# A two-layer graph network: weights split by two engines, and the first four steps in another order

## The chip, the core and the metric

The kernel runs on one core of a Trainium2 chip. The metric is the device time of one launch in microseconds (us), here the median of 3 runs. A core has five engines that run side by side: TensorE (PE, matrix products; its weight loads are listed as PEld), VectorE (DVE), ScalarE (ACT), GpSimd (POOL) and SyncE (SP), which in this kernel only issues DMA transfers. Each engine takes its instructions in the order of the program and waits on semaphores for what other engines produce.

## The reference

For each of N = 128 graphs g with C = 128 nodes and D = 512 features (cut to what matters):

```python
h = relu(layernorm(x))                              # [C, 512]
H = (adj != 0); w = adj[0]                          # incidence, weights of the hyperedges
Dn = 1 / (H @ w); Be = 1 / H.sum(axis=0)            # 0 where the sum is 0
def conv(x, W, b): return Dn * (H @ (Be * (H.T @ (x @ W.T)))) + b
n = layernorm(relu(conv(h, W1, b1))) * gamma + beta # [C, 1024]
x = x + conv(n, W2, b2) + h                         # layer 0
h = relu(layernorm(x))
agg = (adj @ h) / max(adj.sum(-1), 1e-6)
out = x + relu(concat(h, agg) @ W.T)                # layer 1, W is [512, 1024]
```

x is [128, 128, 512], adj [128, 128, 128], all float32. The products with W1, W2 and W must be nearly exact in float32.

## The kernel before

All weights stay in SBUF. [...]each operand of the three large products is split: h is the operand scaled down a little, l what is left (times 4096 in a weight), and d the difference of the two (l - h in a weight). A product is then h.h + l.l in one PSUM bank (`pm`) and d.d in another (`pd`), 8 or 16 matmuls and 4 or 8 more, combined on the way out. The weights, twelve chunks of 128x1024 (some halved), are split once, in the first steps; the raw weights lie in buffers that the loop will use later (`t1`, `h1`, `A` and so on). `DOWN` is 1 - 2^-13, `ONE_UP` 1 + 2^-12. Blank lines are left out here.

```python
class Chunks:
    def __init__(self, w, k, n, tag):
        self.raw = (pool if tag in "rA" else left).tile([P, n, 512], FP, tag=tag, name="raw")
        self.h, self.l, self.d = (w[m][:, k : k + n].bitcast(FR) for m in "hld")
    def high(self):
        copy(self.h, self.raw, AF.Copy, scale=DOWN)
    def low(self, eng):
        eng.tensor_tensor(self.l, self.raw, self.h, SUB)
    def scale(self, eng=nc.scalar):
        if eng is nc.scalar:
            copy(self.l, self.l, AF.Copy, scale=4096.0)
        else:
            eng.tensor_scalar(self.l, self.l, 4096.0, None, MUL)
    def rest(self, eng):
        eng.tensor_tensor(self.d, self.l, self.h, SUB)

W2_TILES = {6: (1, "h1"), 7: (1, "h2"), 0: (1, "h3"), 1: (1, "A"), 2: (2, "t1"), 4: (2, "t2")}
def load_w2(k):
    n, tag = W2_TILES[k]
    c = RAW[2, k] = Chunks(w2, k, n, tag)
    for j in range(Q):
        nc.sync.dma_start(
            out=c.raw[B * j : B * (j + 1)],
            in_=w2t.rearrange("(j k a) o -> j a k o", j=Q, a=B)[j, :, k : k + n])
def scale_w2(k):
    for i in range(W2_TILES[k][0]):
        t = RAW[2, k].raw[:, i, :]
        nc.vector.tensor_scalar(t, t, vector_of(1, k + i), None, MUL)

def beta_row(k):
    if not BETA:
        BETA[0] = small_bank("pc")
    n = W2_TILES[k][0]
    for i in range(n):
        nc.tensor.matmul(BETA[0], vector_of(0, k + i).to_broadcast([P, P]), RAW[2, k].raw[:, i, :],
                         start=(k + i == 6), stop=(k + i == 5))
```

Per graph: `incidence` and `node_matrix` make the graph operators, `mean_operator` that of layer 1.

```python
def mean_operator(g):
    a = ADJ.pop(g)
    deg = pool.tile([P, 1], FP, tag="deg", name="deg", bufs=2)
    nc.vector.tensor_reduce(deg, a, AX.X, ADD)
    nc.vector.tensor_scalar(deg, deg, EPS_DEG, None, MAX)
    nc.vector.reciprocal(deg, deg)
    nc.vector.tensor_scalar(a, a, deg, None, MUL)
    ADJ[g] = a

def incidence(g):
    HT[g] = at = pool.tile([P, P], FP, tag="ht", name="adjt")
    nc.vector.transpose(at, ADJB.pop(g))
    SB[g] = sb = pool.tile([P, P + 1], FP, tag="sb", name="sb")
    nc.vector.tensor_copy(sb[:, P : P + 1], at[:, 0:1])
    nc.vector.tensor_scalar(at, at, 0.0, None, ALU.not_equal)
    cnt = pool.tile([P, 1], FP, tag="cnt", name="cnt", bufs=2)
    nc.vector.tensor_reduce(cnt, at, AX.X, ADD)
    nc.vector.tensor_scalar(cnt, cnt, 1.0, None, MAX)
    nc.vector.reciprocal(cnt, cnt)
    nc.vector.tensor_scalar(sb[:, :P], at, cnt, None, MUL)
def node_matrix(g):
    ps = small_bank("ps_s")
    nc.tensor.matmul(ps[:, : P + 1], HT.pop(g), SB.pop(g), start=True, stop=True)
    S[g] = pool.tile([P, P], FP, tag="s", name="s", bufs=4)
    copy(S[g], ps[:, :P], AF.Copy)
    inv = pool.tile([P, 1], FP, tag="inv", name="inv", bufs=2)
    w = ps[:, P : P + 1]
    nc.vector.tensor_scalar(inv, w, TINY, None, MAX)
    nc.vector.reciprocal(inv, inv)
    DN[g] = dn = pool.tile([P, 2], FP, tag="dinv", name="dinv", bufs=6)
    nc.vector.scalar_tensor_tensor(dn[:, 0:1], w, 0.0, inv, ALU.is_gt, MUL)
    nc.vector.tensor_scalar(dn[:, 1:2], dn[:, 0:1], ONE_UP, None, MUL)
...
def product(left, w, k0, kk, main, name, between=None):
    wr = [w[m].bitcast(FR) for m in "hld"]
    pm, pd = bank(name + "m"), bank(name + "d")
    for i in range(2):
        for k in range(kk):
            nc.tensor.matmul(pm, left[i](k), wr[i][:, k0 + k, :], start=(i == 0 and k == 0),
                             stop=(i == 1 and k == kk - 1))
    main(pm)
    if between:
        between()
    for k in range(kk):
        nc.tensor.matmul(pd, left[2](k), wr[2][:, k0 + k, :], start=(k == 0),
                         stop=(k == kk - 1), skip_group_check=True)
    return pd
...
def conv1_weights(g, half):
    if half == 0:
        R[g] = pool.tile([P, DH], FP, tag="r", name="r")
    cols = HALVES[half]
    r, dn = R[g][:, cols], DN[g]
    PR[g, half] = product(Z[g], w1, KD * half, KD,
                          lambda pm: copy(r, pm, AF.Copy, scale=dn[:, 1:2]), "r")
def conv1_out(g, half):
    cols = HALVES[half]
    r, dn = R[g][:, cols], DN[g]
    nc.vector.scalar_tensor_tensor(r, PR.pop((g, half)), dn[:, 0:1], r, MUL, ADD)
    nc.gpsimd.tensor_tensor(r, r, b1_bc[:, cols], ADD)
```

The left operands of conv2 and layer 1 are turned by a round trip through DRAM (`n_scratch` to `nb`, `h_scratch` to `hb`: one store, four loads) and a transpose on VectorE; then ScalarE makes h, GpSimd l, VectorE d (`split_high`). The order is written by hand. One step of the loop works on several graphs at once; `do(f, g)` runs f for graph g if there is such a graph:

```python
def step(s, extra={}, done=()):
    def do(f, g, *a):
        do(aggregate, s - 3)
    do(layer1_low, s - 3)
    do(conv2_bias, s - 2)
    do(conv1_weights, s, 0)
    do(conv1_out, s, 0)
    do(layer1_rest, s - 3)
    do(residual, s + 1)
    do(mean_operator, s)
    do(mean_out, s)
    do(conv1_weights, s, 1)
    do(conv1_out, s, 1)
    do(conv2_nodes, s - 2)
    do(conv2_out, s - 2)
    do(inner_turn, s - 1)
    do(conv1_nodes, s + 1)
    do(layer1_sums, s - 2)
    do(inner_high, s - 1)
    do(inner_low, s - 1)
    do(scales, s - 2, 3)
    do(mean_in, s)
    do(conv1_high, s + 1)
    do(layer1_mean, s - 3)
    do(layer1_norm, s - 2)
    do(layer1_trip_out, s - 2)
    do(conv1_low, s + 1)
    do(conv1_rest, s + 1)
    do(layer1_mean_out, s - 3)
    do(layer1_self, s - 3)
    do(inner_sums, s)
    do(inner_rest, s - 1)
    do(layer1_trip_in, s - 2)
    do(layer1_self_main, s - 3)
    do(scales, s, 2)
    do(incidence, s + 2)
    do(inner_norm, s)
    do(inner_out, s)
    do(finish, s - 3)
    do(load_adjb, s + 4)
    do(load_adj, s + 1)
    do(inner_in, s)
    do(load_x, s + 3)
    do(x_sums, s + 2)
    do(layer1_turn, s - 2)
    do(scales, s + 2, 1)
    do(conv2_main, s - 1)
    do(x_norm, s + 2)
    do(conv2_weights_out, s - 1)
    do(layer1_high, s - 2)
    do(mean_transpose, s)
    do(node_matrix, s + 2)
```

(Inside conv2_weights, between its two banks, stands `aggregate` of s - 3; it is called through `between`, and without conv2_weights by itself.) The first steps are written out instead:

```python
def split_w3(*cs):
    for c in cs:
        RAW[3, c].high()
        RAW[3, c].low(nc.vector)
    for c in cs:
        RAW[3, c].scale()
        RAW[3, c].rest(nc.gpsimd)

def head():
    copy(eps_root, eps, AF.Sqrt)
    load_x(0)
    load_adjb(0, nc.scalar)
    for half in range(2):
        for i in range(2):
            load_w1(half, i, nc.sync)
    load_affine()
    load_bias(b1_bc, b1)
    load_adjb(1)
    load_x(1)
    load_bias(b2_bc, b2)
    for k in (6, 7, 0, 1):
        load_w2(k)
    load_adj(0)
    x_sums(0)
    incidence(0)
    scales(0, 1)
    RAW[1, 0, 0].high()
    x_norm(0)
    node_matrix(0)
    RAW[1, 0, 1].high()
    RAW[1, 0, 0].low(nc.vector)
    RAW[1, 0, 1].low(nc.gpsimd)
    conv1_nodes(0)
    RAW[1, 0, 0].scale()
    conv1_high(0)
    RAW[1, 0, 1].scale()
    conv1_low(0)
    conv1_rest(0)
    RAW[1, 0, 0].rest(nc.vector)
    RAW[1, 0, 1].rest(nc.gpsimd)
    RAW[1, 1, 0].high()
    RAW[1, 1, 1].high()
    RAW[1, 1, 0].low(nc.vector)
    RAW[1, 1, 1].low(nc.gpsimd)
    RAW[1, 1, 0].scale()
    conv1_weights(0, 0)
    RAW[1, 1, 1].scale()
    RAW[1, 1, 0].rest(nc.vector)
    RAW[1, 1, 1].rest(nc.gpsimd)
    residual(0, nc.vector)
    conv1_out(0, 0)
    load_x(2)
    load_w2(2)
    load_w2(4)
    incidence(1)
    x_sums(1)
    conv1_weights(0, 1)
    node_matrix(1)
    scales(1, 1)
    x_norm(1)
    conv1_out(0, 1)
    load_adjb(2)
    load_adjb(3)
    incidence(2)
    for k in (6, 7, 0, 1):
        beta_row(k)
    conv1_nodes(1)
    conv1_high(1)
    for k in (2, 4):
        beta_row(k)
    for k in (6, 7, 0, 1):
        scale_w2(k)
    inner_sums(0)
    conv1_low(1)
    conv1_rest(1)
    residual(1, nc.vector)
    scales(0, 2)
    inner_norm(0)
    inner_out(0)
    for k in (2, 4):
        scale_w2(k)
    beta_out()
    node_matrix(2)
    for k in W2_TILES:
        RAW[2, k].high()
        RAW[2, k].low(nc.vector)
        RAW[2, k].scale(nc.vector)
        if k != 4:
            RAW[2, k].rest(nc.gpsimd)
    mean_operator(0)
    inner_in(0)
    mean_out(0)
    load_adj(1)
    mean_in(0)
    load_w3(0, "h1")
    load_w3(1, "h2")
    load_w3(2, "h3")
    load_x(3)
    load_adjb(4)
    conv1_weights(1, 0)
    conv1_out(1, 0)
    x_sums(2)
    conv1_weights(1, 1)
    scales(2, 1)
    x_norm(2)
    conv1_out(1, 1)
    inner_turn(0)
    inner_high(0)
    inner_low(0)
    conv1_nodes(2)
    conv1_high(2)
    RAW[2, 4].rest(nc.vector)
    inner_rest(0)
    conv2_weights(0, lambda: None)
    inner_sums(1)
    conv1_low(2)
    conv1_rest(2)
    scales(1, 2)
    inner_norm(1)
    inner_out(1)
    mean_operator(1)
    residual(2)
    incidence(3)
    node_matrix(3)
    conv2_main(0)
    conv2_weights_out(0)
    conv2_bias(0)
    mean_out(1)
    load_adj(2)
    x_sums(3)
    scales(3, 1)
    x_norm(3)
    inner_in(1)
    mean_transpose(0)
    mean_in(1)
    split_w3(0, 1, 2)
    load_w3(3, "h1")
    load_w3(4, "h2")
    load_w3(5, "h3")
    load_x(4)
    load_adjb(5)
    # then step(2) with the rest of W3, and step(3), step(4), ... up to step(N + 2)
```

Of the kernel before, what the change touches and what calls it, by code (L numbers as in the profile page):

```python
# [23 lines left out]
def gnn_kernel(  # L24
# [33 lines left out]
    P = 128  # L58
# [35 lines left out]
    def parts(tag):  # L94
        return {m: const.tile([P, KH, 512], FP, name=tag + m) for m in "hld"}

    w1, w2, w3 = parts("w1"), parts("w2"), parts("w3")
    RAW = {}

    class Chunks:  # L100


        def __init__(self, w, k, n, tag):
            self.raw = (pool if tag in "rA" else left).tile([P, n, 512], FP, tag=tag, name="raw")
            self.h, self.l, self.d = (w[m][:, k : k + n].bitcast(FR) for m in "hld")

        def high(self):
            copy(self.h, self.raw, AF.Copy, scale=DOWN)

        def low(self, eng):  # L110
            eng.tensor_tensor(self.l, self.raw, self.h, SUB)

        def scale(self, eng=nc.scalar):
            if eng is nc.scalar:
                copy(self.l, self.l, AF.Copy, scale=4096.0)  # L115
            else:
                eng.tensor_scalar(self.l, self.l, 4096.0, None, MUL)  # L117

        def rest(self, eng):
            eng.tensor_tensor(self.d, self.l, self.h, SUB)  # L120


    def load_w1(half, i, queue):
        src = w1t.rearrange("(k p) h -> p k h", p=P)
        c = RAW[1, half, i] = Chunks(w1, KD * half + 2 * i, 2, ("r", "t1", "t2", "t3")[2 * half + i])
        queue.dma_start(out=c.raw, in_=src[:, 2 * i : 2 * i + 2, HALVES[half]])

    W2_TILES = {6: (1, "h1"), 7: (1, "h2"), 0: (1, "h3"), 1: (1, "A"), 2: (2, "t1"), 4: (2, "t2")}

    def load_w2(k):  # L130
        n, tag = W2_TILES[k]
        c = RAW[2, k] = Chunks(w2, k, n, tag)
        for j in range(Q):
            nc.sync.dma_start(
                out=c.raw[B * j : B * (j + 1)],
                in_=w2t.rearrange("(j k a) o -> j a k o", j=Q, a=B)[j, :, k : k + n])

    def scale_w2(k):
        for i in range(W2_TILES[k][0]):
            t = RAW[2, k].raw[:, i, :]  # L140
            nc.vector.tensor_scalar(t, t, vector_of(1, k + i), None, MUL)

    def load_w3(c, tag):
        src = wt.rearrange("(n j k a) o -> n j a k o", n=2, j=Q, a=B)
        RAW[3, c] = r = Chunks(w3, c, 1, tag)
        for j in range(Q):
            nc.sync.dma_start(out=r.raw[B * j : B * (j + 1), 0], in_=src[1 - c // KD, j, :, c % KD])
# [5 lines left out]
    def load_affine():  # L153
        for j in range(Q):
            for i, v in enumerate((beta, gamma)):
                nc.gpsimd.dma_start(
                    out=gb[B * j : B * (j + 1), i].rearrange("a (l m) -> a l m", m=2),
                    in_=v.rearrange("(l a) (j m) -> j a l m", a=B, j=Q)[j])

# [6 lines left out]
    BETA = {}  # L166

    def beta_row(k):
        if not BETA:
            BETA[0] = small_bank("pc")  # L170
        n = W2_TILES[k][0]
        for i in range(n):
            nc.tensor.matmul(BETA[0], vector_of(0, k + i).to_broadcast([P, P]), RAW[2, k].raw[:, i, :],
                             start=(k + i == 6), stop=(k + i == 5))
# [76 lines left out]
    def mean_transpose(g):  # L251
        anb = ANT[g]
        ANT[g] = pool.tile([P, P], FP, tag="ant", name="ant", bufs=4)
        nc.vector.transpose(ANT[g], anb)
# [29 lines left out]
    def x_sums(g):  # L284
        H0[g] = pool.tile([P, D], FP, tag="B", name="h0")
        sums((1, g), X[g], H0[g], D)
        spread((1, g), X[g], H0[g], D)
# [14 lines left out]
    def conv1_high(g):  # L302
        Z[g] = z = left.tile([P, 3, KD, P], FP, tag="z", name="z")
        h, l, d = (z[:, i].rearrange("p k c -> p (k c)").bitcast(FR) for i in range(3))
        pz = PZ.pop(g)
        copy(h, pz, AF.Copy, scale=DOWN)  # L306

# [11 lines left out]
    def conv1_rest(g):  # L319
        PZ.pop(g)[1]()  # L320
        z = Z[g].bitcast(FR)
        Z[g] = [lambda k, i=i: z[:, i, k, :] for i in range(3)]


    def product(left, w, k0, kk, main, name, between=None):
        wr = [w[m].bitcast(FR) for m in "hld"]
        pm, pd = bank(name + "m"), bank(name + "d")
        for i in range(2):
            for k in range(kk):
                nc.tensor.matmul(pm, left[i](k), wr[i][:, k0 + k, :], start=(i == 0 and k == 0),  # L330
# [4 lines left out]
        for k in range(kk):  # L335
            nc.tensor.matmul(pd, left[2](k), wr[2][:, k0 + k, :], start=(k == 0),  # L336
# [6 lines left out]
    def conv1_weights(g, half):  # L343
        if half == 0:
            R[g] = pool.tile([P, DH], FP, tag="r", name="r")
        cols = HALVES[half]
        r, dn = R[g][:, cols], DN[g]
        PR[g, half] = product(Z[g], w1, KD * half, KD,
                              lambda pm: copy(r, pm, AF.Copy, scale=dn[:, 1:2]), "r")  # L349

    def conv1_out(g, half):
# [3 lines left out]
        nc.gpsimd.tensor_tensor(r, r, b1_bc[:, cols], ADD)  # L355
# [38 lines left out]
    def split_high(key, a, tags):  # L394
# [8 lines left out]
        def low():  # L403
            SPLIT[key] = part(*l)
            nc.gpsimd.tensor_tensor(SPLIT[key], a, h, SUB)  # L405
# [15 lines left out]
    def inner_low(g):  # L421
        NT[g][0]()
# [331 lines left out]
```

## Time and profile before

| | |
|---|---|
| median of 3 runs | 2566.73 us (2566.22 to 2567.98) |
| span of the profiled execution | 2563.8 us |
| PE busy | 2495.7 us (97%), 11024 matmuls |
| DVE busy | 2062.3 us (80%) |
| ACT busy | 1865.6 us (73%) |
| POOL busy | 1367.8 us (53%) |
| mean granted clock of PE | 0.989 |
| DMA | 311.71 MB, mean 122 GB/s |

A line of the profile's groups reads: line of the program, engine, operation, what it writes <- what it reads, shape and type, xcount | busy us in all and mean ns of one | idle time of the engine just before, and what ended it. `L111` is `Chunks.low`, `L120` is `Chunks.rest`, `L330` and `L336` are the two matmuls of `product`. A line of waits reads: engine, its tile and line <- the engine, tile and line that it waited for: us in total, times, longest.

### The profile page before, as it was taken

What the parts mean: (1) busy time and instruction counts of PE and PEld (TensorE: products, weight loads), DVE (VectorE), ACT (ScalarE), POOL (GpSimd) and SP (SyncE); (2) the same over time, 40 slices, a digit from 0 to 9 for tenths busy, and PEclk for the clock granted to TensorE, in tenths of its full rate; (3) what the DMA queues carried; (4) which work ended last, traced back from release to release, by engine and by line L of the source; (5) the groups of instructions that cost most, each with busy time, mean ns of one, the idle gap of its engine ahead of it and who ended that gap; (6) DMA issues with size and microseconds to landing.
All of it is one profiled execution on the core that took longest, in us unless ns stands there. A gap on an engine that the chain in (4) does not pass through costs nothing.

```text
span 2563.8 us, 38459 instructions
## 1 busy us (share of the span) xinstructions
PE 2495.7 (97%) x11024; PEld 1984.0 (77%) x11024; DVE 2062.3 (80%) x4519; ACT 1865.6 (73%) x3872; POOL 1367.8 (53%) x921
## 2 busy tenths in 40 slices
PE   4799999999999999999999999999999999999997
PEld 3578778778778778778778777787787777877875
DVE  7788888888888887888888878888888888888874
ACT  4677777777777777777777777777777777777773
POOL 4555455455455455555555555555555555555552
PEclk8899999999999999999999999999999999999998
DMA  3343443343343343343443343334343344343332
GB/s 117 115 128 117 128 127 116 125 128 115 128 127 117 128 127 117 125 128 118 124 129 117 120 130 122 119 126 126 119 130 122 117 130 125 116 130 125 116 124 67
DMA packets 410292, 311.71 MB, mean 122 GB/s; under 512 B 177376, under 2 KB 341216, under 8 KB 410080
## 3 DMA queue, kind: packets, MB, share of 16 engines
q1 hardware_dynamic: 409248, 309.19, 38.5%
q8 instruction: 87, 1.43, 0.2%
q14 instruction: 125, 1.02, 0.1%
q10 hardware_dynamic: 576, 0.07, 0.0%
q0 software_dynamic: 256, 0.01, 0.0%
HBM read 166.47 MB, written 142.61 MB: 121 GB/s over the span
## 4 chain that ended last, share of the span: by engine, by line
PE 93%; DVE 2%; ACT 2%; DMA 1%; issue 1%; POOL 1%; SPq 0%; ACTq 0%; DVEq 0%; POOLq 0%
PE gm L330 17%; PE rm L330 17%; PE bm L330 9%; PE am L330 9%; PE rd L336 9%; PE gd L336 9%; PE bd L336 4%; PE py L443 4%; PE ad L336 4%; PE pz L299 4%; PE ad L492 4%; PE ps_s L273 1%; DMA hb<-h_scratch 0%; DVE w2l L117 0%; DMA adjb<-in_adj_dram 0%
## 5 line engine op out<-in xcount | busy, mean ns | idle before, releaser
L405 POOL TENSOR_TENSOR hl<-ht,hh 128x512 fp32r<-128x512 f32 x128 | 165.3, 1291 | 1029.4 <-ACT hh L401 595.9
L217 ACT ACTIVATE h<-x_t 128x512 f32<-128x512 f32 x256 | 161.5, 631 | 343.8 <-DVE x_t L446 327.3
L355 POOL TENSOR_TENSOR r<-r,b_bc 128x512 f32<-128x512 f32 x256 | 386.0, 1508 | 9.2 <-DVE r L354 7.0
L405 POOL TENSOR_TENSOR nl<-nt,nh 128x1024 fp32r<-128x1024 f32 x128 | 308.7, 2411 | 100.3 <-ACT nh L401 99.3
L349 ACT ACTIVATE r<-rm,dinv 128x512 f32<-128x512 f32 x256 | 174.6, 683 | 226.1 <-PE rm L330 226.1
L336 PE MATMUL gd<-w2d,nd 128*128 128x512 f32 x1024 | 307.7, 443 | 3.6 <-DVE nd L410 3.6
L330 PE MATMUL rm<-w1h,z 128*128 128x512 f32 x1024 | 289.5, 405 | 1.4 <-ACT z L306 1.4
L336 PE MATMUL rd<-w1d,z 128*128 128x512 f32 x1024 | 276.5, 391 | 2.2 <-POOL w1d L120 2.2
L330 PE MATMUL rm<-w1l,z 128*128 128x512 f32 x1024 | 276.7, 392 | 2.0 <-ACT w1l L115 2.0
L336 PEld LDWEIGHTS gd<-w2d,nd 128*128 128x128 f32 x1024 | 193.2, 189 | 97.8 <-issue 31.0
L330 PE MATMUL gm<-w2h,nh 128*128 128x512 f32 x1024 | 255.7, 392 | 7.4 <-ACT nh L401 7.4
L330 PE MATMUL gm<-w2l,nl 128*128 128x512 f32 x1024 | 254.6, 391 | 0.0
L228 ACT ACTIVATE h<-x_t,rs 128x512 f32<-128x512 f32 x256 | 208.3, 814 | 32.5 <-DVE rs L224 27.8
L330 PEld LDWEIGHTS gm<-w2h,nh 128*128 128x128 f32 x1024 | 193.8, 189 | 48.2 <-ACT nh L401 7.9
L312 DVE SCALAR_TENSOR_TENSOR z<-z 128x512 fp32r<-128x512 f32 x128 | 226.2, 1768 | 4.4
L330 PEld LDWEIGHTS rm<-w1l,z 128*128 128x128 f32 x1024 | 193.1, 189 | 45.4 <-ACT w1l L115 2.9
L336 PEld LDWEIGHTS rd<-w1d,z 128*128 128x128 f32 x1024 | 192.2, 188 | 45.6 <-POOL w1d L120 3.1
L330 PEld LDWEIGHTS gm<-w2l,nl 128*128 128x128 f32 x1024 | 192.7, 188 | 40.5 <-POOL nl L405 0.4
L330 PEld LDWEIGHTS rm<-w1h,z 128*128 128x128 f32 x1024 | 183.8, 190 | 33.3 <-ACT z L306 1.7
L410 DVE SCALAR_TENSOR_TENSOR hd<-hh,hl 128x512 fp32r<-128x512 f32 x128 | 198.0, 1547 | 4.7 <-POOL hl L405 4.7
L309 DVE TENSOR_TENSOR z<-pz,z 128x512 fp32r<-128x512 f32 x128 | 88.6, 692 | 136.5 <-ACT z L306 136.5
L354 DVE SCALAR_TENSOR_TENSOR r<-rd,dinv,r 128x512 f32<-128x512 f32 x256 | 190.8, 745 | 6.4 <-ACT r L349 1.9
(96 smaller groups left out, 5700.8 us busy)
## 6 DMA issues: line engine op xcount, KB each, us to landing
n_scratch<-r SPq DMA_DIRECT2D x128, 512.0 KB, 2.6
nb<-n_scratch SPq DMA_DIRECT2D x512, 128.0 KB, 2.8
x_t<-in_x_dram SPq DMA_DIRECT2D x128, 256.0 KB, 3.2
h_scratch<-h SPq DMA_DIRECT2D x128, 256.0 KB, 2.0
hb<-h_scratch SPq DMA_DIRECT2D x512, 64.0 KB, 2.0
out_dram<-x_t SPq DMA_DIRECT2D x128, 256.0 KB, 2.0
adj_t<-in_adj_dram SPq DMA_DIRECT2D x128, 64.0 KB, 1.9
an_scratch<-adj_t SPq DMA_DIRECT2D x128, 64.0 KB, 1.7
```

The lines of the kernel that those rows point to most:

```text
L217: copy(junk, src, func, accum_out=sm)
L228: copy(dst, src, func, bias=rs[:, 1:2], scale=rs[:, 0:1])
L299: nc.tensor.matmul(z[:, k * P : (k + 1) * P], H0[g][:, k * P : (k + 1) * P], S[g], start=True, stop=True)
L312: nc.vector.scalar_tensor_tensor(d, h, 2.0**-12, l, MUL, SUB)
L330: nc.tensor.matmul(pm, left[i](k), wr[i][:, k0 + k, :], start=(i == 0 and k == 0), stop=(i == 1 and k == kk - 1))
L336: nc.tensor.matmul(pd, left[2](k), wr[2][:, k0 + k, :], start=(k == 0), stop=(k == kk - 1), skip_group_check=True)
L349: lambda pm: copy(r, pm, AF.Copy, scale=dn[:, 1:2]), "r")
L354: nc.vector.scalar_tensor_tensor(r, PR.pop((g, half)), dn[:, 0:1], r, MUL, ADD)
L355: nc.gpsimd.tensor_tensor(r, r, b1_bc[:, cols], ADD)
L405: nc.gpsimd.tensor_tensor(SPLIT[key], a, h, SUB)
L410: nc.vector.scalar_tensor_tensor(t, h, 2.0**-12, low, MUL, SUB)
L443: nc.tensor.matmul(py, S.pop(g), G.pop(g), start=True, stop=True)
```

## The change

It does five things. The weights are split by ScalarE and VectorE alone; before, GpSimd shared that work. ScalarE multiplies W1 and W3 by 4096 before they are split (for W2 the factor is put into gamma), and VectorE takes l from h and raw in one instruction. A raw half weight lies where its third part d will be, so that it takes no buffer of the loop. The order of the first four steps is new: `head` now reaches into what was step 3, and gives to VectorE some biases and lows that GpSimd does in the loop. In the loop the mean operator of layer 1 is made two steps later, and its buffer is 2 deep instead of 4. The aim is to keep TensorE fed in the first steps.

The diff, cut to its core (cuts are marked; in `head` only the lines of after are shown, as the old head stands above):

```diff
-class Chunks: ...
+class Half:
+    def __init__(self, name):
+        self.name = name
+        self.raw = const.tile([P, KD, 512], FP, tag=name + "d", name=name + "r")
+        self.h, self.l = (const.tile([P, KD, 512], FP, tag=name + m, name=name + m).bitcast(FR)
+                          for m in "hl")
+        self.d = None
+    def up(self, i, eng=nc.scalar):
+        t = self.raw[:, 2 * i : 2 * i + 2]
+            copy(t, t, AF.Copy, scale=4096.0)
+            eng.tensor_scalar(t, t, 4096.0, None, MUL)
+    def high(self, i):
+        c = slice(2 * i, 2 * i + 2)
+        copy(self.h[:, c], self.raw[:, c], AF.Copy, scale=DOWN / 4096.0)
+    def low(self, i):
+        c = slice(2 * i, 2 * i + 2)
+        nc.vector.scalar_tensor_tensor(self.l[:, c], self.h[:, c], -4096.0, self.raw[:, c], MUL, ADD)
+    def rest(self, i, eng=nc.vector):
+        if self.d is None:
+            self.d = const.tile([P, KD, 512], FP, tag=self.name + "d", name=self.name + "d").bitcast(FR)
+        c = slice(2 * i, 2 * i + 2)
+        eng.tensor_tensor(self.d[:, c], self.l[:, c], self.h[:, c], SUB)
+w1, w2, w3 = ([Half(f"w{n}{i}") for i in range(2)] for n in (1, 2, 3))
...
-def load_w2(k): (six tiles, 4 transfers each)
+def load_w2(half): (4 transfers for 4 rows of 512)
+def scale_w2(k, eng): (on ScalarE or VectorE, in place)
...
 def load_affine(): ...
+    nc.gpsimd.tensor_scalar(gb[:, 1], gb[:, 1], 4096.0, None, MUL)
...
-    ANT[g] = pool.tile([P, P], FP, tag="ant", name="ant", bufs=4)
+    ANT[g] = pool.tile([P, P], FP, tag="ant", name="ant", bufs=2)
...
-def conv1_high(g): ...
+def conv1_high(g, early=False): (if early, z lies in h1, h2, h3)
...
 def step(s, ...):
     do(conv1_weights, s, 0)
+    do(conv1_main, s, 0)     (the ACT copy of r, before inside conv1_weights)
...
-    do(mean_operator, s); do(mean_out, s)
+    do(mean_operator, s - 2); do(mean_out, s - 2)
...
-    do(mean_in, s)
+    do(mean_in, s - 2)
...
-    do(load_adj, s + 1)
+    do(load_adj, s - 1)
...
-    do(mean_transpose, s)
+    do(mean_transpose, s - 2)
...
 def head():
     copy(eps_root, eps, AF.Sqrt)
     load_adjb(0, nc.scalar)
     for half in range(2):
         for i in range(2):
+            load_w1(half, i)
     load_affine()
+    load_x(1)
+    load_adjb(1)
     load_bias(b1_bc, b1)
+    for half in range(2):
+        load_w2(half)
     load_bias(b2_bc, b2)
+    load_x(2)
+    load_adjb(2)
     load_adj(0)
     x_sums(0)
+    w1[0].up(0)
+    w1[0].high(0)
+    scales(0, 1)
+    x_norm(0)
+    w1[0].up(1)
+    w1[0].high(1)
     incidence(0)
+    w1[0].low(0)
     node_matrix(0)
     conv1_nodes(0)
+    w1[0].low(1)
+    w1[1].up(0)
+    w1[1].high(0)
+    w1[0].rest(0)
     conv1_high(0)
     conv1_low(0)
     conv1_rest(0)
+    w1[0].rest(1)
+    w1[1].up(1)
+    w1[1].high(1)
+    w1[1].low(0)
+    x_sums(1, "A")
+    scales(1, 1)
+    w1[1].low(1)
+    incidence(1)
+    x_norm(1)
     conv1_weights(0, 0)
+    conv1_main(0, 0)
+    for k in range(2):
+        beta_row(k)
+        scale_w2(k, nc.scalar)
+    w1[1].rest(0)
+    w1[1].rest(1)
+    node_matrix(1)
+    conv1_nodes(1)
     conv1_weights(0, 1)
+    conv1_high(1, True)
     conv1_low(1)
     conv1_rest(1)
+    conv1_main(0, 1)
+    for k in range(2, 4):
+        beta_row(k)
+    conv1_weights(1, 0)
+    conv1_out(0, 0, nc.vector)
+    for k in range(2, 4):
+        scale_w2(k, nc.vector)
+    for i in range(2):
+        w2[0].high(i)
+    conv1_out(0, 1, nc.vector)
+    load_adjb(3)
+    load_w3(0)
+    load_w3(1)
+    for k in range(4, 8):
+        beta_row(k)
+    conv1_weights(1, 1)
+    inner_sums(0)
+    w2[0].low(0)
+    w2[0].low(1)
+    residual(0)
+    for k in range(4, 6):
+        scale_w2(k, nc.vector)
     scales(0, 2)
     inner_norm(0)
     inner_out(0)
+    for k in range(6, 8):
+        scale_w2(k, nc.vector)
+    incidence(2)
+    x_sums(2)
+    scales(2, 1)
+    w2[1].high(0)
+    w2[1].low(0)
+    x_norm(2)
+    node_matrix(2)
+    conv1_nodes(2)
+    w2[1].high(1)
+    w2[1].low(1)
+    conv1_high(2)
+    conv1_low(2)
+    conv1_rest(2)
+    conv1_main(1, 0)
+    conv1_main(1, 1)
     beta_out()
     inner_in(0)
     load_x(3)
     load_adjb(4)
+    load_x(4)
+    load_adjb(5)
     inner_turn(0)
     inner_high(0)
+    w3[0].up(0)
+    w3[0].high(0)
+    conv1_out(1, 0, nc.vector)
+    inner_low(0, nc.vector)
+    conv1_out(1, 1, nc.vector)
+    conv1_weights(2, 0)
+    conv1_weights(2, 1)
+    for i in range(2):
+        w2[0].rest(i)
+    residual(1)
     inner_sums(1)
+    w2[1].rest(0)
     scales(1, 2)
     inner_norm(1)
     inner_out(1)
+    w3[0].up(1)
+    w3[0].high(1)
+    w2[1].rest(1)
+    inner_rest(0)
+    conv2_weights(0, lambda: None)
     residual(2)
     incidence(3)
     x_sums(3)
     scales(3, 1)
     x_norm(3)
+    node_matrix(3)
+    conv1_nodes(3)
+    conv2_main(0)
+    conv2_weights_out(0)
+    conv2_bias(0, nc.vector)
+    conv2_nodes(0)
+    conv1_high(3, True)
+    conv1_main(2, 0)
+    conv1_main(2, 1)
+    conv1_low(3)
+    conv1_rest(3)
+    conv1_weights(3, 0)
+    conv1_weights(3, 1)
     inner_in(1)
+    conv2_out(0)
+    conv1_out(2, 0, nc.vector)
+    layer1_sums(0)
+    inner_turn(1)
+    conv1_out(2, 1, nc.vector)
+    inner_high(1)
+    scales(0, 3)
+    inner_low(1, nc.vector)
+    layer1_norm(0)
+    layer1_trip_out(0)
+    w3[0].low(0)
+    w3[1].up(0)
+    w3[1].high(0)
+    inner_rest(1)
+    conv2_weights(1, lambda: None)
+    inner_sums(2)
+    w3[0].low(1)
+    scales(2, 2)
+    conv2_main(1)
+    inner_norm(2)
+    conv2_weights_out(1)
+    conv2_bias(1, nc.vector)
+    conv2_nodes(1)
+    conv2_out(1)
+    inner_out(2)
+    layer1_trip_in(0)
+    mean_operator(0)
+    mean_out(0)
+    load_adj(1)
+    w3[1].low(0)
+    w3[1].up(1)
+    w3[1].high(1)
+    w3[1].low(1)
+    residual(3)
+    incidence(4)
+    x_sums(4)
+    scales(4, 1)
+    layer1_turn(0)
+    layer1_high(0)
+    layer1_low(0, nc.vector)
+    x_norm(4)
+    node_matrix(4)
+    layer1_rest(0)
+    w3[0].rest(0)
+    w3[0].rest(1)
+    inner_in(2)
+    mean_in(0)
+    w3[1].rest(0)
+    w3[1].rest(1)
     mean_transpose(0)
+    load_adjb(6)
+    load_x(5)
 with tc.manual_schedule():
     head()
+    step(3, done=(conv1_weights, conv2_bias, conv2_nodes, conv2_out,
+                  layer1_low, layer1_rest))
+    for s in range(4, N + 3):
         step(s)
```

## The prediction

> **What bounds the kernel now.** The page comes first: the busy line and the 40 slices of 64 us.
>
> ```profile
> PE 2495.7 (97%) x11024; PEld 1984.0 (77%) x11024; DVE 2062.3 (80%) x4519; ACT 1865.6 (73%) x3872; POOL 1367.8 (53%) x921
> ...
> PE   4799999999999999999999999999999999999997
> ...
> PEclk8899999999999999999999999999999999999998
> ```
>
> TensorE is the bound, and only slices 1, 2 and the last show holes. The waits of TensorE from 120 to 2500 us are one line:
>
> ```profile
> PE py L443 <- POOL g L439: 0.4, 1, 0.4
> ```
>
> So a step of the loop lasts as long as its matmuls: the first `rm` starts at 1012.59 and, one step later, at 1031.84, 19.25 us for one g. What the other engines save there is worth nothing. I cut the first 120 us into stages (columns: stage, length, then PE, PEld, DVE, ACT, POOL busy us with counts, clock, DMA share, GB/s):
>
> ```profile
> 10.00:30.00 20.00, 11.26 (x34) 7.49 (x34) 15.72 (x20) 11.72 (x18) 13.42 (x5) 0.96 0.58 163
> 30.00:48.00 18.00, 16.32 (x52) 9.83 (x52) 15.03 (x39) 10.90 (x20) 3.26 (x3) 0.85 0.09 33
> 48.00:64.00 16.00, 2.02 (x8) 1.78 (x8) 15.72 (x18) 3.89 (x9) 10.60 (x6) 0.53 0.18 49
> 64.00:80.00 16.00, 13.45 (x53) 10.25 (x53) 9.97 (x28) 10.11 (x22) 7.06 (x4) 0.94 0.49 143
> 80.00:100.00 20.00, 8.95 (x29) 6.78 (x28) 15.72 (x20) 14.45 (x30) 15.69 (x11) 0.75 0.33 86
> 100.00:120.00 20.00, 16.89 (x65) 12.85 (x65) 12.56 (x31) 11.00 (x24) 11.57 (x9) 0.83 0.37 110
> ```
>
> From 48 to 64 us VectorE is full (15.72 of 16) and TensorE has 2 us of work. The waits of TensorE up to 122 us name the rest:
>
> ```profile
> PE ps_s L273 <- DVE sb L268: 17.0, 4, 9.9
> PE pz L299 <- ACT h L228: 15.2, 1, 15.2
> PE gm L330 <- ACT nh L401: 7.4, 1, 7.4
> PE gd L336 <- DVE nd L410: 3.6, 1, 3.6
> PE rd L336 <- POOL w1d L120: 2.2, 2, 1.6
> ```
>
> The 15.2 us before `pz` is a chain: ScalarE's `h` waited for `rs` on VectorE, and `rs` stood in VectorE's program behind six W2 chunks (44 to 58 us).
>
> How much can be won? At full clock a 128x512 matmul costs 0.2275 us (four in 0.91). Work up to the start of `gm` of g=2 at 120.04: conv1 of g=0 to 3, conv2 of g=0 and 1, layer 1 of g=0 are 24 matmuls each, 7 x 5.46 = 38.2; beta rows 16 records x 0.45 = 7.2; five `pz` at 0.9 = 4.5; two `py` at 0.9 = 1.8; five `ps_s` 1.2. Together 52.9. So 120.0 - 52.9 = **67 us are lost in the head**. The change removes no matmul, so all it can save lies in these 67 us. The first `ps_s` at 9.88 us waits for the first adjacency, which comes no earlier, so over 57 us is out of reach, and 51 us (2%) would need a head with almost no hole.
>
> [...]
>
> ```profile
> 16.40 3.01 POOL L120 TENSOR_TENSOR w1d<-w1l,w1h 128x1024 fp32r<-128x1024 f32 x1 [1.17 <-DMA raw<-in_w2t_dram]
> ```
>
> ```profile
> 17.30 3.19 DVE L111 TENSOR_TENSOR w1l<-raw,w1h 128x1024 fp32r<-128x1024 f32 x1
> ```
>
> GpSimd ends at 19.41, VectorE at 20.49, 1.08 later; alone the same instruction takes 1.22 (at 11.79). [...] Here the first four `rm` at 14.64 us took 2.07, later ones 1.07[...].
>
> **The change part by part.** Durations are the uncontended ones of the head, start to start: VectorE 128x1024 1.2, 128x512 0.68; ScalarE 0.97 and 0.55.
>
> 1. *Splitting.* GpSimd lost 17 instructions to splitting (2 low, 15 rest; 33 us busy: 6.5+5.7+6.9+3.2+10.9). [...] ScalarE multiplies W1 and W3 by 4096 before, not between, the parts: the same 0.97 each, but the old chain low, scale, rest (VectorE to ScalarE and back) becomes high, low, rest. For W2, 4096 rides on gamma: the 4.6+4.3 us of VectorE scaling at a mean of 1.14 and 2.17 fall away.
>
> 2. *VectorE's new head,* up to the mean_transpose that ends it: 12 chunks x (low+rest) = 24 x 1.2 = 28.8; six W2 rows x 0.42 = 2.5; five incidences x 1.7 = 8.5 (8.04 to 9.74); five node matrices x 0.75 = 3.75; nine scales x 0.4 = 3.6; conv1 splits 4 x 1.35 = 5.4; six conv1_out with bias (now VectorE's) x 1.35 = 8.1; turn, low, rest of two inner operands 6 x 1.2 = 7.2; conv2 out and bias 2 x 1.33 = 2.7; conv2_out 2 x 0.7 = 1.4; layer 1 turn, low, rest 2.0; mean operator, transpose, beta_out 1.8. **Sum 75.8 us.** ScalarE, summed likewise, has 59, TensorE 46.6 up to `pz` of g=4. VectorE is thus the bound of the new head: 8 (adjacency lands) + 75.8 = 84 us at the earliest.
>
> 3. *Its idle time.* I walked the new order by hand, each instruction after the later of its engine and its input. VectorE waits for W1's second high, for the beta rows ahead of the W2 scaling (a few us around 28 to 34), for ScalarE's sums ahead of scales, and for the n round trip (store 2.6, four issues 1.7, load 2.8 = 7.1 us, mostly filled). That adds 8: 92.
>
> 4. *Contention left.* GpSimd keeps four residuals of 2 x 1.26 us = 10 us in the head, and starts each as soon as its input is there. If half of it blocks VectorE: 5. **Head end at about 97.** What then stands between it and `gm` of g=2 is two conv1_out, a mean operator, inner_turn (3.5), ScalarE's high (1.0), some 5 us: `gm` of g=2 starts at about **102**, against 120.0. On the way I expect the first `gm` at 50 (64.0), `py` of g=0 at 63 (79.3), `gm` of g=1 at 72 (88.6), `pz` of g=4 at 90 (113.7). TensorE has those 5 us filled with layer 1 of g=0.
>
> 5. *Order within a step, the mean operators.* The load, the operator and the transpose move by two steps but keep their places in a step: the same instructions, the transpose now one step ahead of its `aggregate`, before three. Nothing in the loop; in the last two steps they are extra, about 1 us of VectorE each, where VectorE waits 1 to 4 us at a time: under 1 us.
>
> Sum: 120 - 102 = 18 saved, less 1.3 for the first steps after the head and the tail: 16.7. 2566.7 - 16.7 = **2550 us**.
>
> **Rivals.** *A: VectorE takes over as the bound and eats the gain.* It gets the biases, lows and rests of GpSimd. For: it is busy 86.5 of 120 us already, and 15.72 of 16 in the worst stage. Against: much of that is blocked time (3.19 for 1.22, 1.37 for 0.43). If all 10 us of residuals and 15 us of idling fall on it, `gm` of g=2 starts at 114: 2561. *B: the DMA round trips and the queue set the head.* The load of the sixth blocked adjacency waits for a buffer that incidence(3) frees, and inner_out(1) stands behind it in the same queue; g=1's turn would come late, perhaps 3 to 6 us: 2553 to 2556. *C: the loop suffers.* Each 0.1 us per step is 12.8 us; against it speaks the 0.4 us of waits in 2380 us and VectorE at 82% there. 2565 to 2580, unlikely. *D: it goes as planned,* VectorE never idle, nothing blocked: head 86, `gm` at 91: 2538.
>
> **Range and chances.** D and A bound it: 2539 to 2562. More than 2% faster (below 2515) would need 51 of the 57 us within reach, when VectorE's sum alone forbids more than some 30; over 2% slower needs the loop to break. So 0.01 / 0.98 / 0.01; that it is faster at all I put at 0.9.
>
> **What would show it.** Right: GpSimd busy 15 to 20 us of the first 95 (66 of 120 before), no 3 us VectorE split, VectorE over 80% busy from 10 to 95 us with TensorE waiting mainly for VectorE, `gm` of g=2 near 102, step still 19.25. Wrong: TensorE waiting for `nb` or `hb` landings (B), `gm` of g=2 beyond 112 (A), a new wait in the loop (C).

## The result and the profile after

| | before | after |
|---|---|---|
| median of 6 runs | 2566.94 us | 2545.1 us |
| ratio, 95% interval | 1 | 0.9918, 0.9905 to 0.9931 |
| span of the profiled execution | 2563.8 us | 2541.1 us |
| `gm` of g=0 starts at | 64.03 | 48.87 |
| `py` of g=0 | 79.27 | 63.72 |
| `gm` of g=1 | 88.60 | 71.90 |
| `pz` of g=4 | 113.67 | 88.57 |
| `gm` of g=2 | 120.04 | 99.70 |

The change won 21.8 us, 0.8%; foretold were 16.7, 2550 us with a range of 2539 to 2562. The mark that the prediction aimed at is the start of `gm` of g=2, in before (first line) and in after:

```profile
120.04 1.98 PE L330 MATMUL gm<-w2h,nh 128*128 128x512 f32 x8
```

```profile
99.70 1.20 PE L337 MATMUL gm<-w20h,nh 128*128 128x512 f32 x4 [1.65 <-ACT nh L408]
```

A line of this kind has the start in us, the length in us, and in brackets how long the engine stood idle before it and what ended that. `fp32r` in such lines is the type float32r, `FR` in the code. The page of after, busy time and slices:

```profile
PE 2490.4 (98%) x11024; PEld 1982.9 (78%) x11024; DVE 2057.7 (81%) x4523; ACT 1866.5 (73%) x3864; POOL 1324.0 (52%) x898
...
PE   6899999999999999999999999999999999999997
...
PEclk9899999999999999999999999999999999999998
```

Only the first slices of TensorE have changed: the first from 4 to 6, the second from 7 to 8. What TensorE waited for longest up to 122 us (us in total, times, longest):

```profile
PE ps_s L272 <- DVE sb L267: 17.7, 3, 11.0
PE pz L298 <- ACT s L274: 5.4, 5, 1.9
PE gd L343 <- DVE nd L417: 3.4, 1, 3.4
PE py L450 <- DVE g L446: 2.8, 2, 1.7
PE gm L337 <- ACT nh L408: 1.7, 1, 1.7
```

The 15.2 us before `pz` and the 7.4 before `gm` are gone. Of the 17.7 us in the first line, 11.0 are the wait for the first adjacency at the start. Up to 95 us TensorE waits after that another 13.6 us for VectorE and 6.8 for ScalarE. By stages of after (length, then PE, PEld, DVE, ACT, POOL busy with counts, clock, DMA share, GB/s):

```profile
20.00:40.00 20.00, 17.02 (x65) 11.00 (x63) 17.90 (x40) 13.75 (x25) 4.83 (x3) 1.00 0.78 185
40.00:60.00 20.00, 14.48 (x58) 10.78 (x58) 17.61 (x31) 14.47 (x24) 3.75 (x2) 0.93 0.28 80
60.00:80.00 20.00, 16.70 (x60) 12.35 (x60) 15.27 (x24) 14.92 (x26) 2.54 (x2) 0.82 0.18 64
80.00:100.00 20.00, 10.83 (x36) 8.42 (x36) 17.42 (x37) 8.11 (x20) 4.55 (x4) 0.66 0.31 78
100.00:120.00 20.00, 18.92 (x83) 14.48 (x82) 16.40 (x36) 14.53 (x32) 11.32 (x9) 1.00 0.39 120
```

VectorE is busy for 15 to 18 of each 20 us; TensorE's largest hole is left from 80 to 100 us, where the clock is down to 0.66 too. GpSimd, busy for 8 to 16 us of each 20 in before, has 2.5 to 5 until the head ends.

Of the 22.7 us between the two spans, 20.3 are there when `gm` of g=2 starts, and 18.8 when that product ends (the next `ps_s` at 126.37 and 107.53): of the 1.5 lost, 1.1 are a wait of its second half for GpSimd's `nl` in after. In this pair of executions 2.5 us come in the loop: six steps mostly last 115.40 us in after and 115.52 in before. The rest, 1.4 us, comes in the last steps. In a second execution of after (the run `after_again` below) the span is 2545.1 us and the same `ps_s` starts at 108.32, so only some 0.7 of the 18.7 us to before come behind it.

### The profile page after: what moved, and what is told of

The parts are those of the page before. It is cut to its first block, busy times and chain, and to the rows that moved or that the text cites. A ratio compares the mean times of both kernels' runs of the same rounds, so it can differ in the third digit from the quotient of the medians.

```text
span 2541.1 us, 38324 instructions
## 1 busy us (share of the span) xinstructions
PE 2490.4 (98%) x11024; PEld 1982.9 (78%) x11024; DVE 2057.7 (81%) x4523; ACT 1866.5 (73%) x3864; POOL 1324.0 (52%) x898
## 4 chain that ended last, share of the span: by engine, by line
PE 94%; DMA 2%; DVE 1%; ACT 1%; issue 1%; POOL 1%; SPq 0%; DVEq 0%; POOLq 0%; ACTq 0%
PE gm L337 18%; PE rm L337 18%; PE bm L337 9%; PE am L337 9%; PE rd L343 9%; PE gd L343 9%; PE bd L343 4%; PE py L450 4%; PE ad L343 4%; PE pz L298 4%; PE ad L499 4%; PE ps_s L272 1%; DMA x_t<-in_x_dram 0%; DMA hb<-h_scratch 0%; DMA w11r<-in_w1t_dram 0%
## 5 line engine op out<-in xcount | busy, mean ns | idle before, releaser
L343 PE MATMUL gd<-w20d,nd 128*128 128x512 f32 x512 | 189.3, 491 | 3.4 <-DVE nd L417 3.4
L210 ACT ACTIVATE h<-x_t,nm 128x512 f32<-128x512 f32 x256 | 185.4, 724 | 8.3
L298 PEld LDWEIGHTS pz<-s,h 128*128 128x128 f32 x1024 | 136.5, 195 | 65.6 <-issue 58.9
L293 POOL TENSOR_TENSOR x_t<-x_t,b_bc 128x512 f32<-128x512 f32 x128 | 168.2, 1314 | 20.4 <-DMA adjb<-in_adj_dram 10.5
L292 POOL TENSOR_TENSOR x_t<-x_t,h 128x512 f32<-128x512 f32 x128 | 164.1, 1282 | 27.8 <-ACT h L227 27.7
L227 ACT ACTIVATE r<-r,rs 128x1024 f32<-128x1024 f32 x128 | 158.9, 1241 | 6.3 <-DVE rs L223 1.9
L446 POOL TENSOR_TENSOR g<-g,c 128x512 f32<-128x512 f32 x126 | 162.6, 1291 | 0.0
L388 DVE STREAM_TRANSPOSE nt<-nb 128x1024 f32<-128x1024 f32 x128 | 157.6, 1232 | 5.8 <-DMA nb<-n_scratch 4.7
L337 PE MATMUL bm<-w30h,hh 128*128 128x512 f32 x512 | 154.1, 424 | 4.4 <-ACT hh L408 4.4
L417 DVE SCALAR_TENSOR_TENSOR nd<-nh,nl 128x1024 fp32r<-128x1024 f32 x128 | 154.7, 1209 | 2.7 <-POOL nl L412 2.7
```

The source lines that it names most:

```text
L210: copy(junk, src, AF.Square, bias=NM[key], accum_out=ss)
L227: copy(dst, src, func, bias=rs[:, 1:2], scale=rs[:, 0:1])
L293: eng.tensor_tensor(X[g], X[g], b2_bc, ADD)
L298: nc.tensor.matmul(z[:, k * P : (k + 1) * P], H0[g][:, k * P : (k + 1) * P], S[g], start=True, stop=True)
L337: nc.tensor.matmul(pm, left[i](k), right(i, k), start=(i == 0 and k == 0), stop=(i == 1 and k == kk - 1))
L343: nc.tensor.matmul(pd, left[2](k), right(2, k), start=(k == 0), stop=(k == kk - 1), skip_group_check=True)
```

## The experiments

Each kernel is after or before with one edit. All ratios are against before on the same chip; "marks" are starts in the profiled execution. A mark is one reading: in the two executions of after, `gm` of g=2 starts at 99.70 and 100.50, that of g=0 at 48.87 and 51.01. The letters in the expectations name theories of that experiment, not the rivals of the prediction.

### Which engine splits, in the old order

```diff
-RAW[1, 0, 1].low(nc.gpsimd)      +RAW[1, 0, 1].low(nc.vector)
-RAW[2, k].rest(nc.gpsimd)        +RAW[2, k].rest(nc.vector)
 (and so for every low and rest)
```

> The kernel before, with its order, its buffers and its arithmetic, but every low and rest of the weights on VectorE instead of GpSimd. [...] If the engine is only one part and the order of the steps is the larger one (B, mine), VectorE gets some 14 us of work (17 instructions) and loses some 12 to 15 us of blocking, so that the head hardly moves: 2560 to 2566. gm of g=2 then starts at 115 to 120 us (120.0 before, 99.7 after).

Measured: 2565.27 us, ratio 0.9993 (0.9985 to 1.0002); `gm` of g=2 at 119.46. As B (the engine is only one part) expected: with the old order the engine alone is worth nothing that the interval can tell from zero, though `py` of g=0 comes at 76.8 instead of 79.3. The early gain is lost again before g=2.

### The mean operators alone

```diff
-do(mean_operator, s)             +do(mean_operator, s - 2)
 (load_adj, mean_out, mean_in, mean_transpose likewise; those of g=0, 1 leave the head)
```

> The kernel before with only the mean operators (load, operator, both transfers, transpose) two steps later. Theory B: the head loses three operators and transposes on VectorE (3 x 1.1 us and up to 1 us of blocking), and some queue time, so gm of g=2 starts 2 to 4 us earlier and the time is 2563 to 2565. Rival: a step of the loop gets shorter too (the trace of after has 19.233 us for 19.253); if the mean operators do that, the step of this kernel is 19.23 as well, and 2.5 us more are gained: 2561. The other rival, that they matter for nothing: 2567.

Measured: 2559.73 us, ratio 0.9973 (0.9963 to 0.9984), 4 to 9.5 us. `gm` of g=2 at 116.48, 3.6 us earlier, as expected; the most frequent step is 19.24 us, for 19.25 in before. The time is better than all three theories expected, more than the mark and the step add up to (3.6 + 120 x 0.01 = 4.8), but its interval holds that sum. The profiled execution was the slowest of the eight (2563.99 us), with a span only 1.9 us below that of before, so its marks do not explain the median.

Part of the earlier mark is a wait on SyncE. In before the store of `h` of g=0 goes out at 101.99 us, and VectorE then waits 4.09 us for `hb`; here it goes out at 96.84, and the wait is 0.47 (before first, then this kernel):

```profile
100.14 1.75 SPq L185 DMA_DIRECT2D anb<-an_scratch  x4
101.99 0.60 SPq L366 DMA_DIRECT2D h_scratch<-h  x1
```

```profile
94.90 1.84 SPq L185 DMA_DIRECT2D anb<-an_scratch  x4
96.84 0.38 SPq L366 DMA_DIRECT2D h_scratch<-h  x1
```

The load of an operator (`anb`) stands ahead of that store in both, but goes out 5.2 us earlier here.

### The rests on GpSimd, in the new order

```diff
-def rest(self, i, eng=nc.vector):
+def rest(self, i, eng=nc.gpsimd):
```

> The kernel after with all twelve rests (d = l - h) on GpSimd, nothing else changed. If VectorE's work is the bound and the engines can share it (C), VectorE loses 12 x 1.15 = 13.8 us and gm of g=2 comes at 88 to 93 us: about 2535. If they lock each other out (A and B), GpSimd takes 12 x 2.4 = 29 us or more[...], and gm of g=2 comes at 103 to 110 us: 2549 to 2555.

Measured: 2558.22 us, ratio 0.9964 (0.9951 to 0.9977), 13 above after; `gm` of g=2 at 114.11. That the engines can share the work (C) falls, and it is worse than A and B expected. VectorE's groups in the first 110 us of this kernel (count | busy us, mean ns | idle before):

```profile
L147 DVE TENSOR_SCALAR w21r<-w21r,gb 128x512 f32<-128x512 f32 x4 | 6.0, 1522 | 0.0
...
L261 DVE TENSOR_SCALAR adjt<-adjt 128x128 f32<-128x128 f32 x5 | 4.9, 974 | 0.2
...
L223 DVE TENSOR_TENSOR rs<-nm,rs 128x1 f32<-128x1 f32 x9 | 4.3, 478 | 0.3
```

and the same in the first 97 us of after:

```profile
L147 DVE TENSOR_SCALAR w21r<-w21r,gb 128x512 f32<-128x512 f32 x4 | 1.8, 481 | 0.0
...
L261 DVE TENSOR_SCALAR adjt<-adjt 128x128 f32<-128x128 f32 x5 | 1.1, 227 | 0.2
...
L223 DVE TENSOR_TENSOR rs<-nm,rs 128x1 f32<-128x1 f32 x9 | 1.4, 159 | 0.3
```

VectorE was given 13.8 us less to do and `gm` of g=2 came 14.4 us later. From 11 us to the end of the head (the transpose of the mean operator, at 107.3 us and 94.6 in after) VectorE is busy for 76.4 us instead of 72.4, so what is left of its work lasts some 18 us longer. Its waits for other engines there grew too, from 8.9 to 17.7 us. Three of the groups, of which two have nothing to do with weights and one scales rows of W2, cost 10.9 us more than in after. GpSimd's subtractions take 2.3 to 2.6 us each. Here the instruction of one column, 0.16 us on average in after, takes 2.16 and ends at 43.3 us, as the second of GpSimd's two does:

```profile
41.17 2.16 DVE L223 TENSOR_TENSOR rs<-nm,rs 128x1 f32<-128x1 f32 x1
```

```profile
38.24 5.07 POOL L122 TENSOR_TENSOR w20d<-w20l,w20h 128x1024 fp32r<-128x1024 f32 x2 [9.97 <-DVE w20l L116]
```

### Twice the rests on VectorE

```diff
+for _ in range(2):
     eng.tensor_tensor(self.d[:, c], self.l[:, c], self.h[:, c], SUB)
```

> The kernel after with every rest computed twice on VectorE: 12 more instructions of 1.15 us, 13.8 us in all, the result is unchanged. If VectorE bounds the new head (B), nearly all of it shows, less what falls into the 9 us in which it idles: gm of g=2 at 109 to 113 us, time 2555 to 2559. If round trips or TensorE bound it, less than half shows: below 2551.

Measured: 2559.96 us, ratio 0.9972 (0.9961 to 0.9983), 15 above after and just above the range. Its `gm` of g=2:

```profile
113.21 2.07 PE L338 MATMUL gm<-w20h,nh 128*128 128x512 f32 x4 [4.44 <-ACT nh L409]
```

13.5 us later than in after, for 13.8 us of work. VectorE's work is what the new head lasts for.

### VectorE's idle time filled

```diff
 incidence(3); x_sums(3)
+w3[0].low(0)
 scales(3, 1); x_norm(3)
+w3[0].low(1)
 ...
-w3[0].low(0); w3[1].up(0); w3[1].high(0)
 inner_rest(1); conv2_weights(1, ...); inner_sums(2)
-w3[0].low(1)
+w3[0].rest(0)
 scales(2, 2); inner_norm(2); conv2_main(1)
+w3[0].rest(1); mean_operator(0)
 conv2_weights_out(1); conv2_bias(1, nc.vector)
+w3[1].up(0); w3[1].high(0); w3[1].low(0)
 (the same calls are taken away further down; w3[1].low(1) behind layer1_high(0))
```

> The kernel after with the same instructions, but five splits of W3 and the first mean operator moved in VectorE's order into stretches in which the trace of after shows it idle (57.6 to 60.5, 72.9 to 77.6, 79 to 80.4 us), and the sums of g=2 ahead of W3's second half on ScalarE. If VectorE's sum plus its idle time sets the end of the head (B), about 5 of the 9 us of idle time are filled and gm of g=2 starts at 94 to 96 us (99.7): 2539 to 2541. If the waits only move elsewhere (round trip of h, ScalarE), gm stays at 98 to 100: 2544 to 2546.

Measured: 2540.28 us, ratio 0.9899 (0.9883 to 0.9916). Three of the moved instructions on VectorE, and the `gm` of g=2 on TensorE:

```profile
57.56 1.22 DVE L116 SCALAR_TENSOR_TENSOR w30l<-w30h,w30r 128x1024 fp32r<-128x1024 f32 x1
...
72.06 1.22 DVE L122 TENSOR_TENSOR w30d<-w30l,w30h 128x1024 fp32r<-128x1024 f32 x1
...
77.69 1.23 DVE L116 SCALAR_TENSOR_TENSOR w31l<-w31h,w31r 128x1024 fp32r<-128x1024 f32 x1 [0.46 <-ACT w31h L112]
```

```profile
93.32 1.20 PE L337 MATMUL gm<-w20h,nh 128*128 128x512 f32 x4
```

6.4 us earlier than in after with the same instructions, a little more than expected. VectorE's waits for other engines, from 11 us to the end of the head, fell from 8.9 to 2.9 us, and that end came at 88.3 instead of 94.6. Once more beside an unchanged after:

> The kernel after, unchanged, on the same chip as the others: 2545, ratio 0.9918, gm of g=2 at 99 to 100 us.

> The kernel with the filled idle time once more, beside after on the same chip: 4 to 6 us below it, 2539 to 2541, gm of g=2 at 93 to 94 us.

Measured: 2546.23 us for after (0.9917, 0.9902 to 0.9932), 2539.2 for this one (0.9891, 0.9877 to 0.9906); `gm` of g=2 at 100.50 and 93.62. That is 7.0 us, more than the 4 to 6 expected, and every run of the filled kernel here (2538.65 to 2540.42) lies below every run of after (2543.9 to 2547.54). It is the fastest kernel of the study.

### No residuals beside the head

```diff
 def residual(g, eng=nc.gpsimd):
+    if g < 4:
+        return
```

> The kernel after without the residual additions (x + h0 and + b2, on GpSimd) for the first four graphs; it leaves these sums out of the output, nothing else. GpSimd then does next to nothing in the head. In the trace of after VectorE's instructions beside the residuals last 3.6 us longer than elsewhere. If that blocking lies on the path (A, B): gm of g=2 at 96 to 98 us, 2541 to 2543. If it falls into idle time: no change, 2545.

Measured: 2543.11 us, ratio 0.9908 (0.9894 to 0.9923), and

```profile
96.14 1.19 PE L339 MATMUL gm<-w20h,nh 128*128 128x512 f32 x4 [3.12 <-ACT nh L410]
```

3.6 us earlier than in after. This kernel leaves the first four residuals out of its output; they take no TensorE time, so the 3.6 us, read from one execution, are what four pairs of GpSimd additions cost VectorE. The time agrees with that (2.0 us less) but its interval does not part it from after, and the profiled execution was the fastest of the four (2540.04 us).

### The buffer t2

```diff
-for k in W2_TILES:
+for k in (4, 6, 7, 0, 1, 2):
```

> The kernel before with only the order of the six W2 tiles changed: the raw tile that lies in t2 is split first, so that t2 comes free some 9 us earlier. In the trace of before the load of nb was issued at 55.4 us, when t2 came free, and the store had ended by 46. Rival D: the buffer that the raw weights occupied held the round trip up, and the first gm with it; then gm of g=0 starts earlier than 64 us by several us and the time falls to 2560 or less. B: VectorE is busy with W2 until 58 us in any case and inner_turn stands behind it in program order: nb is early, gm of g=0 stays within 1 us of 64.0, the time within 2 us of 2567.

Measured: 2567.17 us, ratio 1.0001 (0.9992 to 1.001). The load of `nb` is issued at 45.1 us instead of 55.4, and `gm` of g=0 starts at 63.20 instead of 64.03. That this buffer held the first `gm` up (D of this experiment) falls: the round trip was hidden behind VectorE.

### The new arithmetic in the old order

```diff
-copy(self.h, self.raw, AF.Copy, scale=DOWN)     (high; then low, scale, rest)
+copy(self.raw, self.raw, AF.Copy, scale=4096.0) (up; then high)
+nc.vector.scalar_tensor_tensor(self.l, self.h, -4096.0, self.raw, MUL, ADD)
 (all on ScalarE and VectorE; gamma x 4096 for W2)
```

> The kernel before, its order and buffers kept, with the splitting of after: times 4096 ahead on ScalarE (in gamma for W2), low in one VectorE instruction, all lows and rests on VectorE. Against the run with only the engine changed it drops VectorE's 8.9 us of W2 scaling (5 us when not blocked) and the wait of ScalarE between low and rest. If splitting is what pays, this alone gives most of the 22 us: 2548 to 2552. If the order and the buffers carry most of it (B): gm of g=0 at 56 to 60 us, gm of g=2 at 112 to 118, 2558 to 2564.

Measured: 2565.67 us, ratio 0.9995 (0.9986 to 1.0004). `gm` of g=0 at 56.95, as B expected, `py` of g=0 at 72.17, 7.1 us earlier than in before; but `gm` of g=2 at 119.46, where 112 to 118 was expected, and the time misses its 2558 to 2564 as well. So the win is there and is eaten. Where, SyncE's transfers and VectorE's instructions of this kernel show (start us, us, what):

```profile
98.11 1.75 SPq L182 DMA_DIRECT2D anb<-an_scratch  x4
99.95 0.38 SPq L363 DMA_DIRECT2D h_scratch<-h  x1
```

```profile
97.78 0.30 DVE L251 STREAM_TRANSPOSE ant<-anb 128x128 f32<-128x128 f32 x1
...
105.52 0.71 DVE L378 STREAM_TRANSPOSE ht<-hb 128x512 f32<-128x512 f32 x1 [5.50 <-DMA hb<-h_scratch]
106.16 0.12 DVE L220 RECIPROCAL rs<-sd 128x1 f32<-128x1 f32 x1
106.31 0.16 DVE L221 TENSOR_TENSOR rs<-nm,rs 128x1 f32<-128x1 f32 x1
106.42 0.69 DVE L433 TENSOR_TENSOR g<-gd,g 128x512 f32<-128x512 f32 x1
```

`h` of g=0 was ready at 90.7, but its store stands in SyncE's queue behind the load of `anb`, which waits until the transpose at 97.8 has freed that one buffer. Then VectorE waits 5.5 us for `hb`, with `g` behind it, and `py` of g=1 with that.

### That queue wait taken away in two ways

```diff
-ANT[g] = pool.tile([P, P], FP, tag="anb", name="anb")
+ANT[g] = pool.tile([P, P], FP, tag="anb", name="anb", bufs=2)
```

> The run with the old order and the new arithmetic, and one thing more: the tile anb has two buffers. In that run h of g=0 was ready at 90.7 us, but its store was issued at 99.95, behind the load of anb (98.1) in the same queue, and that load waited for mean_transpose of g=1 on VectorE (97.8) to free anb. VectorE then stood before the turn of h until 105.5. If this wait is what ate the 7 us won by the first py (E: the queue), the store is issued at 91 to 92, py of g=1 comes at 102 to 105 (110.5), gm of g=2 at 111 to 114 (119.5), the time is 2557 to 2561. If VectorE's own work is the wall (B alone), gm of g=2 stays at 117 to 120: 2564 to 2566.

Measured: 2561.09 us, ratio 0.9976 (0.9968 to 0.9985), 4.6 below the run without the second buffer. The store of `h` went out at 93.35; `gm` of g=2 at 116.36. The wait is real, but it was worth 3 us of marks and not 7 (111 to 114 was expected): `py` of g=1 still starts at 109.15, where 102 to 105 was expected, because TensorE had to do conv1 of g=3 first, and that began only here:

```profile
101.35 0.80 PE L270 MATMUL ps_s<-sb,adjt 128*128 128x129 f32 x2 [5.58 <-DVE sb L265]
```

The incidence stands behind the last two W3 chunks on VectorE (96.0 to 99.1), whose raw rows were issued in a third round, while the second was split (first line below, 87.8 us). In after all loads of W3 are issued by 29.2 us (second fence). But the third round is not what these chunks waited for last. Its loads landed 1.7 to 2.0 us after their issue, the last by 93.4; ScalarE came to the rows only at 94.74 (third fence), right behind other work of its own, and VectorE waited 2.48 us for what ScalarE made of them:

```profile
87.79 3.57 SPq L143 DMA_DIRECT2D raw<-in_wt_dram  x8
```

```profile
25.48 1.85 SPq L140 DMA_DIRECT2D w30r<-in_wt_dram  x4
27.38 1.86 SPq L140 DMA_DIRECT2D w31r<-in_wt_dram  x4
```

```profile
94.74 0.61 ACT L108 ACTIVATE raw<-raw 128x512 f32<-128x512 f32 x1
```

The second way is the one of the change, the new arithmetic with late mean operators:

> The old order and the new arithmetic, with the mean operators two steps later, as in after. If the queue is the wall (E), this removes the same wait, and three mean operators and transposes from VectorE besides: gm of g=2 at 108 to 112 us, 2554 to 2558, so the two changes together win 9 to 13 us where each alone won 1 and 7. If the two simply add: 2558 to 2559. What then is missing to after (2545) belongs to the buffers of the raw W3 and the order.

Measured: 2559.58 us, ratio 0.9972 (0.9962 to 0.9982); `gm` of g=2 at 114.16. The expectation of 108 to 112 and of 2554 to 2558 was missed. By marks the two win 5.9 us together (0.6 and 3.6 alone); by time 7.2, no more than the mean operators alone (6.9).

## Why the prediction was right, and where it was off

**The bound.** That VectorE's work and waits set the new head held: 13.5 of 13.8 added us came out at `gm` of g=2, and filling 6.0 us of VectorE's waits gave 6.4 back. Of the signs, GpSimd is busy 18.1 us of the first 95 (15 to 20 foretold) and VectorE 73.7 of the 85 us from 10 to 95 (87%; over 80% foretold). That all there is to win lies in the head's 67 us held for most of it, 18.8 of 22.7 us.

**The sum.** The five marks were foretold at 50, 63, 72, 90 and 102 us and came at 48.9, 63.7, 71.9, 88.6 and 99.7. Term by term: the head starts at 9.1 us, when the first adjacency has landed, not at 8. The end of the head (the transpose of the mean operator ends at 94.6) was put at 97. Idle time of VectorE between 11 and 95 us: 8.9 (8). Lengthening beside the residuals: 3.6 by the durations and 3.6 by experiment (5). What remains of the span, 94.6 - 9.1 - 8.9 - 3.6 = 73.0, is the work, put at 75.8: the 1.2 us per split was rounded up (two in a row take 2.27), which over 24 of them is 1.6 of the 2.8 us. From head to `gm`: 5.1 (5).

**The terms that were mis-sized.** The mark was put 2.3 us too late, by the terms above. The larger miss is the last term, "less 1.3 for the first steps after the head and the tail". The first steps do cost it (20.3 become 18.8), but after them came 3.9 us of gain in this pair of executions, and 3.0 by the medians (21.8 less 18.8), not zero. How firm that is stays open, as the second execution of after shows some 0.7. The most frequent step lasts 19.23 us in all new-order kernels, 19.24 in the two old-order ones with late mean operators and 19.25 in the other old-order ones, so "nothing in the loop" looks wrong by 0.02 us per step. But the mean step from `py` of g=4 to that of g=120 is 19.246 and 19.264 us in the two executions of after, 19.268 in before, and 19.279 in the old order with only late mean operators. That scatter is as large as the effect, and no run settles what shortens a step. The end can't be read either: the last `py` to `py` took 18.2 us in one execution of after and 19.4 in the other.

**Part 1, splitting.** No weight split on VectorE took over 1.8 us in after (up to 3.19 in before). The split of 1.22 us at 11.79, which the prediction calls alone, had one of GpSimd beside it from 12.13 on; but in after, where GpSimd idles from 63.0 to 95.4, a tensor_tensor of that size at 70.64 takes 1.22 too. But what the engine is worth depends on the order. Lows and rests on GpSimd or VectorE: 2567 or 2565 in the old order; rests alone, 2558 or 2545 in the new one. In the old order something else, later, holds whatever is won early; in the new one VectorE's program sets the head, and what GpSimd blocks there shows in the time.

**Part 5, the mean operators**, was the step that I misjudged in kind. I took them for a neutral matter of the loop. By themselves, in the old order, they are worth 4 to 9.5 us: three operators less on VectorE in the head, and an operator's load that no longer holds the store of `h` up (101.99 to 96.84 us). No run parts these two, and none has the new order with early mean operators.

**The rivals.** A (VectorE eats the gain) was the right bound with too large a size. B (queue and round trips) is not what limits after, where the first `nb` was issued at 39.0 and VectorE turned it at 45.0 without a wait; but it is part of what limited before (4.09 us before `hb`). C (the loop suffers) was wrong: no new wait shows in the loop. D's 2538 (VectorE never idle, nothing blocked; its head of 86 us is 2 more than the sum of 84) was nearly reached by the filled kernel, at 2540 and 2539.

**What stays open.** The old order with the new arithmetic and late mean operators is at 2559.6, after at 2545. These 14 us belong to the order of the first four steps, with the work that it moves from GpSimd to VectorE, and to the place of the raw weights together; no run parts these. So it is shown what bounds the new head, but not which part of the change made most of the gain. The third round of W3 loads does not show a share of the buffers, since those chunks waited last for ScalarE.

## What to carry to other kernels

When one engine's instruction stream is the bound of a stretch, add up its work and its idle gaps there, and move work that has long been ready into the gaps: the same instructions in another order were worth 5 to 7 us here. An early win that does not arrive later has met another wait: look for the in-order queue, DMA issue included, in which an urgent instruction stands behind one that waits for a buffer (`h` ready at 90.7 and stored at 99.95 in the old order with the new arithmetic). Before giving work to GpSimd beside a full VectorE, look at what VectorE's short instructions take while it runs (478 ns instead of 159 on average for one column, with the rests on GpSimd).

## What the runs showed of the hardware

In the new head GpSimd's 128x1024 subtractions cost VectorE more than they took off it: 13.8 us of work less, some 18 us of longer instructions, and `gm` of g=2 14.4 us later. Even a tensor_tensor of one column took 478 ns on average instead of 159, and a 128x128 tensor_scalar 974 instead of 227, while GpSimd's own took 2.3 to 2.6 us. That so short instructions pay so much was not in my sum.
